# Spare transposes, a borrowed buffer and a new order in the setup of an adaptive-norm attention and expert block

## The chip, the core and the metric

The kernel runs on one core of a Trainium2 chip. The metric is the device time of one execution in microseconds (us). The engines are named as in the profile: PE is TensorE's matrix multiply and PEld its load of the stationary operand, DVE is VectorE, ACT is ScalarE, POOL is GpSimd, and SP is SyncE, whose queue (SPq) issues most transfers.

## What is computed

x is 2 x 2048 tokens of width 256. Everything is float32.

```
mod = (silu(c) @ wmod).reshape(B, 6, 1, 256)        # sa, ca, ga, sb, cb, gb
ga, gb = sign * max(abs, 0.25)
h   = layernorm(x) * (1 + ca) + sa
q, k, v = split(h @ Wqkv)                           # 16 heads of 64
p   = softmax(q k' / 8, each query sees itself and the 127 tokens before it)
x   = x + ga * ((p v) @ Wout)
h   = layernorm(x) * (1 + cb) + sb
the two best of 8 experts per token, at most 640 tokens per expert and choice:
y  += (relu(h W1[e] + b1[e]) W2[e] + b2[e]) * probability
x   = x + gb * y
```

## The kernel before, in words

**Split products.** Each float32 product is made of three matmuls in the fp32r format: a value is split into an upper part (a copy to fp32r, `upper` L129, on ACT) and a lower part (value minus upper, `lower` L133, on DVE or, for Wout, on POOL). `passes` (L225) multiplies upper by upper, upper by lower and lower by upper. So a weight is of use only once both parts are there.

**Setup.** SP loads c, the first x, the first third of wmod, and two of the six pieces of Wqkv (`weights` L359; piece n is q, k or v by n % 3, first or second half of the heads by n // 3). POOL writes the constants, ident for the transposes first. The setup makes silu(c) (sg, L436 to L439), transposes it (tp_c L442), multiplies it with wmod (`modulation` L451), copies the row to SBUF (wide, L464), and turns it to columns (mod_cols L469, cols L473). In the meantime `norm(0)` (L238), a generator moved on by `next(first)`, normalizes the first group (z), transposes it (tp_h L254), and scales it (hT L260) into its upper and lower part hh and hl.

**Pieces of weights.** Each `weights(n)` is a generator of three steps: load, `high(n)`, `low(n)`. The raw pieces share two buffers (tag raw of the pool stage), so the load of piece n+2 stands in `low(n)` (L388), behind the lower part that frees its buffer. Pieces 6 and 7 are the two halves of Wout.

**Attention.** A group is 256 tokens; there are 16, eight per batch. The 64 iterations of the loop (L1156) take two pairs of heads each, in a pipeline: iteration w makes q and k for the pairs of w+1 (`project_qk`), v (`project_v`), the scores of its own pairs (`scores`), packs them (`pack`), takes the maximum and the exponentials (`exps`); `normalize`, `turn`, `unpack`, `values` and `out_project` of a pair follow one to three iterations later. All matmul outputs of this part come from a ring of six PSUM banks (`bank`, L91), so a bank is written again only when the reader of the sixth output before it is done.

**Pack.** The scores of a head stand in one bank: per tile of 128 queries a block of own keys and a block of the keys before. In the first group of a batch (groups 0 and 8) the first tile has no keys before; DVE adds the mask `after` to it (L588). For the second tile ACT copies the own block (L595), and DVE copies over it, where the mask `within` says so, the block before (L596). Two heads make a pack, one bank each.

**Order.** Up to L1266 the order on every engine is the order of the program, written by hand. Work beside the pipeline is placed by strings such as "1A": iteration 1, point A. The points of an iteration are, in order, A, B, M, H, C, S, V (`go`, L1149). SECOND (L1108) places the rest of the setup (`second_half`, L491): the remaining weight pieces, the next x, the transposes of the gate weights (tp_g), the second and third part of the modulation with their rows (written to memory and read back, L531 to L535). `clear` (L537) writes zeros to the experts' buffers, two transfers per iteration of the first ones. After L1266 the order comes from a scheduler; there the experts run.

Of the kernel before, what the change touches and what calls it, by code (L numbers as in the profile page):

```python
# [8 lines left out]
FP = mybir.dt.float32  # L9
FR = mybir.dt.float32r  # L10
I32 = mybir.dt.int32
AF = mybir.ActivationFunctionType
ALU = mybir.AluOpType
# [4 lines left out]
P = 128  # L18
# [10 lines left out]
def adaln_block_kernel(  # L29
# [18 lines left out]
    nc = tc.nc  # L48
    B, S, D = x.shape
    DH = 64  # L50
    H = wqkv.shape[1] // 3 // DH
    HD = H * DH
# [7 lines left out]
    ND = D // P  # L60
# [6 lines left out]
    TS = SBT * P  # L67
# [20 lines left out]
    stage = ctx.enter_context(tc.tile_pool(name="stage", bufs=2))  # L88
    ring = {}

    def bank(name, shape=(P, 512)):  # L91
        return ring["pool"].tile(list(shape), FP, tag="ring", name=name, bufs=ring["bufs"])

    ident = const.tile([P, P], FP, name="ident")
# [26 lines left out]
            in_=rowd[b : b + 1, 0:3, :].rearrange("a i d -> a (i d)").to_broadcast([P, 3 * D]),  # L121
        )

    def load(src, shape, name):
        raw = stage.tile(shape, FP, tag="raw", name=f"raw_{name}")
        nc.sync.dma_start(out=raw, in_=src)
        return raw

# [62 lines left out]
    wq = bigw.tile([P, 2, ND, 3 * HD], FR, tag="big", name="wq")  # L191
# [8 lines left out]
    def load_x(g):  # L200
        xg = xp.tile([P, SBT, D], FP, tag="x", name=f"x_{g}")
        nc.sync.dma_start(
            out=xg, in_=xf[g * TS : (g + 1) * TS, :].rearrange("(t p) d -> p t d", p=P)
        )
        return xg
# [29 lines left out]

    qs, vs, xs, hs = {}, {}, {}, {}

    def norm(g):  # L238

        b = g // GPB  # L240
        xg = xs[g]
        mv, rs = norm_stats(xg, f"a{g}")
        yield
        z = wk.tile([P, SBT, D], FP, tag="t2", name=f"z_{g}")
        for t in range(SBT):
            nc.vector.tensor_scalar(
                z[:, t, :], xg[:, t, :], mv[:, t, 0:1], rs[:, t : t + 1],
                ALU.subtract, ALU.mult,
            )
        yield  # L250
        tp = bank(f"tp_h{g}")
        for k in range(ND):
            for t in range(SBT):
                nc.tensor.transpose(  # L254
                    tp[:, k * TS + t * P : k * TS + (t + 1) * P], z[:, t, k * P : (k + 1) * P], ident
                )
        yield
        hT = wk.tile([P, ND, TS], FP, tag="t2", name=f"hT_{g}")
        for k in range(ND):
            nc.vector.tensor_scalar(  # L260
                hT[:, k, :], tp[:, k * TS : (k + 1) * TS],
                cols[:, 1, k, b : b + 1], cols[:, 0, k, b : b + 1], ALU.mult, ALU.add,
            )
        hh = wk.tile([P, ND, TS], FR, tag="hh", name=f"hh_{g}")
        hl = wk.tile([P, ND, TS], FR, tag="hl", name=f"hl_{g}")
        if g:
            yield
            nc.scalar.copy(hh, hT)
            yield
        else:  # L270

            for k in range(ND):
                nc.scalar.activation(
                    hh[:, k, :], tp[:, k * TS : (k + 1) * TS], AF.Identity,
                    scale=cols[:, 1, k, b : b + 1], bias=cols[:, 0, k, b : b + 1],
                )
            yield
        nc.vector.tensor_tensor(hl, hT, hh, ALU.subtract)  # L278
        hs[g] = (hh, hl)
        yield  # L280
# [25 lines left out]
    def part(dh, dl, src):  # L306
        nc.scalar.copy(dh, src)
        nc.vector.tensor_tensor(dl, src, dh, ALU.subtract)  # L308
# [27 lines left out]
    first = norm(0)  # L336
# [7 lines left out]
    def load_mod(m):  # L344

        wms[m] = sp.tile([P, ND, 2 * D], FP, tag="wm", name=f"wm_{m}")
        nc.sync.dma_start(
            out=wms[m],
            in_=wmod.rearrange("(k p) f -> p k f", p=P)[:, :, 2 * m * D : (2 * m + 2) * D],
        )  # L350
# [3 lines left out]
    def columns(n):  # L354

        i, j = divmod(n, 3)
        return slice(j * HD + i * HD // 2, j * HD + (i + 1) * HD // 2)

    def weights(n):  # L359

        raw = load(
            wqkv[:, columns(n)].rearrange("(k p) f -> p k f", p=P), [P, ND, HD // 2], f"wq{n}"
        )
        hi, lo = (wq[:, m, :, columns(n)] for m in range(2))
        scale = None if n % 3 else QSCALE
        yield
        upper(hi, raw, scale)
        yield
        lower(hi, lo, raw, scale)
# [15 lines left out]
    def high(n):  # L385
        next(parts_[n])

    def low(n):  # L388

        next(parts_[n], None)  # L390
        if n + 2 < len(parts_):
            next(parts_[n + 2])

    for n in range(2):
        next(parts_[n])
# [42 lines left out]
    nc.vector.reciprocal(sg, sg)  # L438
    nc.vector.tensor_tensor(sg, sg, cr, ALU.mult)  # L439
    next(first)  # L440
    tp = bank("tp_c")
    nc.tensor.transpose(tp[:, 0 : B * ND], sg, ident[0 : B * ND, 0 : B * ND])  # L442
    scT = sp.tile([P, B, ND], FP, name="scT")
# [7 lines left out]
    def modulation(m):  # L451

        mr = bank(f"mod_{m}")
        for k in range(ND):
            nc.tensor.matmul(
                out=mr[0:B, :], lhsT=scT[:, :, k], rhs=wms[m][:, k, :],
                start=(k == 0), stop=(k == ND - 1),
            )
        return mr


    mr = modulation(0)
    wide2 = sp.tile([B, 2, D], FP, tag="wide", name="wide_0").rearrange("b i d -> b (i d)")
    nc.scalar.copy(wide2, mr[0:B, :])  # L464
    next(first)
    next(first)
    mc = bank("mod_cols")
    for i in range(2 * ND):
        nc.tensor.transpose(  # L469
# [9 lines left out]
    low(0)  # L479
    next(first)  # L480
    high(1)
    part(*project_qk(0, 0, 0))
    low(1)
    high(2)
    part(*project_qk(0, 0, 1))
    low(2)
# [4 lines left out]
    def second_half():  # L491

        for n in range(3, 8):
            if n == 5:
                load_mod(1)
            high(n)
            yield
            low(n)
            if n < 6:
                yield  # L500
        xs[2] = load_x(2)
        yield
        tp = bank("tp_g")
        for k in range(ND):
            nc.tensor.transpose(
                tp[:, k * E : (k + 1) * E], gw[:, k * P : (k + 1) * P], ident[0:E, 0:E]
            )
        nc.tensor.transpose(
            tp[:, ND * E : ND * E + E * NF], b1r, ident[0 : E * NF, 0 : E * NF]
        )  # L510
        nc.vector.tensor_copy(gwT.rearrange("p k e -> p (k e)"), tp[:, 0 : ND * E])
        nc.vector.tensor_copy(b1T, tp[:, ND * E : ND * E + E * NF])
        yield

        for g in range(2):
            mr = modulation(g + 1)
            if g == 0:
                load_mod(2)
            wide = sp.tile([B, 2, D], FP, tag="wide", name=f"wide_{g + 1}")
            gate, plain = (mr[0:B, 0:D], mr[0:B, D:]) if g == 0 else (mr[0:B, D:], mr[0:B, 0:D])  # L520
            nc.vector.tensor_scalar(sgn, gate, 0.0, 2.0, ALU.is_ge, ALU.mult)
            nc.vector.tensor_scalar(sgn, sgn, -1.0, None, ALU.add)
            nc.vector.tensor_tensor(mag, gate, sgn, ALU.mult)
            nc.vector.scalar_tensor_tensor(
                wide[:, g, :], mag, 0.25, sgn, ALU.max, ALU.mult
            )
            if g == 0:
                nc.vector.tensor_copy(wide[:, 1, :], plain)
            else:
                nc.vector.tensor_scalar(wide[:, 0, :], plain, 1.0, None, ALU.add)  # L530
            nc.sync.dma_start(out=rowd[:, 2 * g : 2 * g + 2, :], in_=wide)  # L531
            yield
        load_rows(0)
        for b in range(B):
            nc.sync.dma_start(out=gbr[:, b, :], in_=rowd[b, 3:4, :].to_broadcast([P, D]))  # L535
# [43 lines left out]
    def pack(g, hp):  # L579


        sc = scs.pop((g, hp))
        pm = wk.tile([P, 2, SBT, P], FP, tag="pm", name=f"pm_{g}_{hp}", bufs=4)
        first = g % GPB == 0
        for h in range(2):
            blocks = sc[h].rearrange("p t (n k) -> p (t n) k", n=2)
            if first:
                nc.vector.tensor_tensor(pm[:, h, 0, :], blocks[:, 1, :], after, ALU.add)  # L588
                ts, own, before = slice(1, 2), slice(3, 4), slice(2, 3)
            elif key_blocks(g, 0)[1]:  # L590
                ts, own, before = slice(0, 2), slice(0, 4, 3), slice(1, 3)
            else:
                ts, own, before = slice(0, 2), slice(1, 4, 2), slice(0, 4, 2)
            n = ts.stop - ts.start
            nc.scalar.copy(pm[:, h, ts, :], blocks[:, own, :])  # L595
            nc.vector.copy_predicated(  # L596
                pm[:, h, ts, :],
                within.rearrange("p (a k) -> p a k", a=1).to_broadcast([P, n, P]),
                blocks[:, before, :],
            )  # L600
        pms[g, hp] = pm

# [502 lines left out]
        NG - 2: "0H 1B 1V 2H 2C 2V 3A 3B 3H 3C 3V".split(),  # L1105
        NG - 1: ["0H"],
    }
    SECOND = "0B 0M 0M 0S 1B 1S 1V 2B 2V 3A 3A 3V 3V".split()  # L1108
    places = {}

    def place(work, w, at):
# [269 lines left out]
```

## Time and profile before

| | us |
|---|---|
| median of 3 runs | 1149.95 |
| lowest, highest | 1148.7, 1150.23 |
| the profiled execution, its time | 1148.45 |
| its span, first to last instruction | 1146.7 |
| PE busy | 1077.6 (94%) |
| PE weight loads busy | 991.4 (86%) |
| DVE busy | 874.0 (76%) |
| ACT busy | 678.0 (59%) |
| POOL busy | 587.0 (51%) |

The page gives the span in 40 slices of 28.7 us; a digit is the busy share of an engine in tenths, and the row PEclk is TensorE's granted clock in tenths of full speed. A line of the timeline is start, duration, engine, line of the kernel, operation, output <- inputs, shape and count, and in brackets how long the engine had been idle and what ended that. A line of the waits is the waiting instruction <- the one it waited for, with the sum in us, the number of waits and the longest. A line of the stretches is the stretch, its length, the busy time of PE, PEld, DVE, ACT and POOL with instruction counts, the granted clock, the DMA share and GB/s.

### The profile page before, as it was taken

Reading aid. Unit: us, or ns where it says so; the run is one execution under the profiler, and the core shown is the slowest. Engines: PE = TensorE matmul, PEld = TensorE weight load, DVE = VectorE, ACT = ScalarE, POOL = GpSimd, SP = SyncE. Lnnn points to the kernel's source line nnn. Section 1 sums busy time; section 2 is a strip of 40 time slices with the busy share of each in tenths; the row PEclk is TensorE's granted clock in tenths of the full one; section 3 lists DMA queues with packets and bytes.
Section 4 is the critical chain, followed back from the end, with each engine's and each line's share of the span. In section 5 each row is a group of like instructions: output and inputs, shape, how many; then the busy total and the mean of one; then the engine's idle time right before and its main releaser. Section 6 shows DMA issues by size and latency. Waiting matters only on the chain. (4 is left out here: it accounts for less than half of the span.)

```text
span 1146.7 us, 25186 instructions
## 1 busy us (share of the span) xinstructions
PE 1077.6 (94%) x9238; PEld 991.4 (86%) x9238; DVE 874.0 (76%) x2170; ACT 678.0 (59%) x2099; POOL 587.0 (51%) x767
## 2 busy tenths in 40 slices
PE   6799999999999999999999997788899999999995
PEld 4589999999999889999999996678799999999994
DVE  4667778878878778888888876677678787778773
ACT  3667677777777577777777776433444444344441
POOL 1345375575575555665665666444233525443524
PEclk9899999999999999999999998779999999999998
DMA  4866200000000010010010022233353434343413
GB/s 130 205 147 152 45 30 20 31 30 20 30 30 21 21 48 25 21 36 20 18 36 21 18 61 66 76 99 90 70 140 94 64 106 87 87 83 76 76 50 37
DMA packets 59863, 72.09 MB, mean 63 GB/s; under 512 B 4841, under 2 KB 51186, under 8 KB 59728
## 3 DMA queue, kind: packets, MB, share of 16 engines
q1 hardware_dynamic: 48016, 55.54, 17.1%
q0 software_dynamic: 11712, 14.79, 7.5%
q8 instruction: 80, 1.31, 0.5%
q14 instruction: 55, 0.45, 0.1%
HBM read 40.11 MB, written 32.27 MB: 63 GB/s over the span
## 5 line engine op out<-in xcount | busy, mean ns | idle before, releaser
L230 PE MATMUL pq<-hh,wq 128*128 128x256 f32 x1024 | 217.9, 297 | 7.8 <-DVE wq L135 5.4
L1008 ACT ACTIVATE hm<-ph,b1T 128x256 fp32r<-128x256 f32 (+2 forms) x184 | 99.2, 539 | 212.3 <-PE ph L230 182.3
L619 ACT ACTIVATE pm<-pm,mx 128x128 f32<-128x128 f32 x512 | 204.3, 403 | 15.7 <-DVE mx L605 15.6
L230 PE MATMUL y<-we,hm 128*128 128x256 f32 x1440 | 203.1, 285 | 6.2 <-DVE hm L1010 6.1
L230 PE MATMUL ph<-xT,we 128*128 128x256 f32 (+2 forms) x1104 | 199.2, 320 | 9.0 <-PEq L1314 3.6
L230 PEld LDWEIGHTS y<-we,hm 128*128 128x128 f32 x1440 | 186.9, 190 | 9.6 <-DVE hm L1010 8.3
L653 POOL TENSOR_SCALAR_AFFINE_SELECT pT<-pT 128x512 f32<-128x512 f32 (+1 forms) x128 | 79.8, 624 | 207.1 <-ACT pT L652 207.0
L230 PEld LDWEIGHTS ph<-xT,we 128*128 128x128 f32 x1104 | 168.2, 192 | 13.9 <-issue 4.2
L230 PEld LDWEIGHTS pq<-hh,wq 128*128 128x128 f32 x1024 | 170.8, 194 | 10.3 <-DVE wq L135 5.8
L230 PE MATMUL pq<-hl,wq 128*128 128x256 f32 x512 | 146.7, 287 | 0.6 <-DVE hl L278 0.6
L1009 DVE TENSOR_SCALAR r<-ph,b1T 128x256 f32<-128x256 f32 (+2 forms) x184 | 102.5, 563 | 58.6 <-ACT hm L1008 49.4
L629 POOL TENSOR_TENSOR pm<-pm,rd 128x512 f32<-128x512 f32 x128 | 133.6, 1044 | 26.0 <-DVE rd L627 26.0
L595 ACT COPY pm<-sc 128x256 f32<-128x256 f32 (+1 forms) x256 | 81.0, 362 | 107.0 <-PE sc L571 72.5
L1073 POOL TENSOR_TENSOR ys<-ys,gw 128x256 f32<-128x256 f32 x56 | 47.4, 942 | 171.3 <-DVE ys L1063 168.6
L676 PE MATMUL av<-pT,v 128*64 128x128 f32 (+1 forms) x1472 | 124.5, 317 | 5.2 <-ACT v L326 1.8
L676 PEld LDWEIGHTS av<-pT,v 128*64 128x64 f32 x1472 | 89.7, 138 | 33.2 <-issue 3.5
L596 DVE COPY_PREDICATED pm<-within,sc 128x256 f32<-128x256 int32 (+1 forms) x256 | 96.1, 422 | 24.9 <-ACT pm L595 23.8
L1074 POOL DMA_INDIRECT out_dram<-ys,tok x60 | 97.2, 1620 | 28.0 <-issue 12.1
L571 PE MATMUL sc<-kr,qh 64*128 64x256 f32 (+1 forms) x1024 | 102.5, 294 | 1.4 <-DVE ql L308 1.2
L230 PEld LDWEIGHTS pq<-hl,wq 128*128 128x128 f32 x512 | 99.6, 195 | 0.9 <-DVE hl L278 0.9
L619 ACT ACTIVATION_READ_ACCUMULATOR pm<-pm,mx 128x1 f32 x512 | 99.8, 195 | 0.0
L1010 DVE TENSOR_TENSOR hm<-r,hm 128x256 fp32r<-128x256 f32 (+2 forms) x144 | 95.2, 661 | 5.4
(166 smaller groups left out, 2249.5 us busy)
## 6 DMA issues: line engine op xcount, KB each, us to landing
raw_w<-in_L_ffn_W_dram SPq DMA_DIRECT2D x32, 512.0 KB, 3.7
xbuf<-blank SPq DMA_DIRECT2D x16, 685.0 KB, 10.1
xt<-xbuf SPq DMA_DIRECT2D x7, 822.0 KB, 6.5
xt<-xbuf SPq DMA_DIRECT2D x8, 548.0 KB, 4.9
x<-in_L_attn_x_dram SPq DMA_DIRECT2D x16, 256.0 KB, 2.9
out_dram<-x SPq DMA_DIRECT2D x16, 256.0 KB, 2.2
raw_wq<-in_L_attn_Wqkv_dram SPq DMA_DIRECT2D x6, 512.0 KB, 4.1
wm<-in_L_wmod_dram SPq DMA_DIRECT2D x3, 512.0 KB, 5.3
```

The lines of the kernel that those rows point to most:

```text
L230: nc.tensor.matmul(out=out_, lhsT=a, rhs=b, start=start and n == 0 and i == 0, stop=stop and n == last and i == 2, **kw,)
L571: nc.tensor.matmul(out=sc[h][:, t, lo:], lhsT=q[r, t * P : (t + 1) * P], rhs=kr[r, (0, 1, 0)[i], hp, blk, :], start=(i == 0), stop=(i == 2),)
L595: nc.scalar.copy(pm[:, h, ts, :], blocks[:, own, :])
L596: nc.vector.copy_predicated(pm[:, h, ts, :], within.rearrange("p (a k) -> p a k", a=1).to_broadcast([P, n, P]), blocks[:, before, :],)
L619: nc.scalar.activation(pm[:, h, t, :], pm[:, h, t, :], AF.Exp, bias=mx[:, h, t : t + 1], accum_out=den[:, h, t : t + 1],)
L629: nc.gpsimd.tensor_tensor(pmv, pmv, rd.rearrange("p h (t a) -> p (h t) a", a=1).to_broadcast([P, 2 * SBT, P]), ALU.mult,)
L653: nc.gpsimd.affine_select(out=pT[:, :, t0:, 0, :], in_=own[:, :, t0:, :], pattern=[[0, 2], [0, n], [-1, P]], compare_op=ALU.is_gt, fill=0. ...
L676: nc.tensor.matmul(out=av[h * DH : (h + 1) * DH, q0 : q0 + hi - lo], lhsT=v[:, f0 + h * DH : f0 + (h + 1) * DH], rhs=pT[:, h, lo:hi], star ...
L1008: nc.scalar.activation(hh[:, s], phv, AF.Relu, bias=bias)
L1009: nc.vector.tensor_scalar(r[:, s], phv, bias, 0.0, ALU.add, ALU.max)
L1010: nc.vector.tensor_tensor(hl, r[:, 0:W], hh, ALU.subtract)
L1074: add = nc.gpsimd.indirect_dma_start(out=of, out_offset=bass.IndirectOffsetOnAxis(ap=tok[:, 0:1], axis=0), in_=y, in_offset=None, bounds_c ...
```

## The change

1. `keep_warm(n)` issues n transposes of ident on TensorE into a bank that nothing reads: 11 before tp_c, 3 before the modulation's matmul, 4 before mod_cols, 12 before the first projection.
2. Piece 2 of Wqkv (v, first half) is loaded into the buffer of the first third of wmod, behind the modulation's matmul, no longer behind `low(0)`. So `low(0)` loads piece 3, `low(1)` piece 4, and from `low(3)` on it is piece n+2 as before.
3. `low(1)` moves ahead of the first pair's `part`: on DVE ahead of ql_0. `low(4)` moves from point S of iteration 0 to point C: on DVE ahead of its packs.
4. wide is copied by DVE, no longer by ACT. For the first group hh is copied from hT by ACT, no longer computed by ACT from the bank that DVE reads for hT.
5. In a pack, the copy of ACT is issued first, and DVE's mask add goes to the other head's bank; both predicated copies stand at the end. In other groups than a batch's first, the order on each engine stays as it was.
6. The third x is loaded in iteration 1, ahead of the load of wmod. The second half of Wout (upper and lower part) moves from iteration 2 to 3, the lower part of its first half from point B to H of iteration 2, the gate transposes and the second part of the modulation from iteration 3 to 4, the third part and the rows from iteration 3 to 5. Clears and rows change places on SP accordingly.

PE's, DVE's, ACT's and POOL's orders differ nowhere else in the hand-ordered part but for the packs of group 8; in the scheduled part about ten matmuls change places with neighbours.

```diff
--- before.py
+++ after.py
@@ -121,8 +121,8 @@
             in_=rowd[b : b + 1, 0:3, :].rearrange("a i d -> a (i d)").to_broadcast([P, 3 * D]),
         )
 
-    def load(src, shape, name):
-        raw = stage.tile(shape, FP, tag="raw", name=f"raw_{name}")
+    def load(src, shape, name, pool=stage, tag="raw"):
+        raw = pool.tile(shape, FP, tag=tag, name=f"raw_{name}")
         nc.sync.dma_start(out=raw, in_=src)
         return raw
 
@@ -235,6 +235,12 @@
 
     qs, vs, xs, hs = {}, {}, {}, {}
 
+    def keep_warm(n):
+
+        tp = bank("idle")
+        for i in range(n):
+            nc.tensor.transpose(tp[:, i % 4 * P : (i % 4 + 1) * P], ident, ident)
+
     def norm(g):
 
         b = g // GPB
@@ -256,6 +262,8 @@
                 )
         yield
         hT = wk.tile([P, ND, TS], FP, tag="t2", name=f"hT_{g}")
+        if g == 0:
+            keep_warm(12)
         for k in range(ND):
             nc.vector.tensor_scalar(
                 hT[:, k, :], tp[:, k * TS : (k + 1) * TS],
@@ -268,12 +276,8 @@
             nc.scalar.copy(hh, hT)
             yield
         else:
-
             for k in range(ND):
-                nc.scalar.activation(
-                    hh[:, k, :], tp[:, k * TS : (k + 1) * TS], AF.Identity,
-                    scale=cols[:, 1, k, b : b + 1], bias=cols[:, 0, k, b : b + 1],
-                )
+                nc.scalar.copy(hh[:, k, :], hT[:, k, :])
             yield
         nc.vector.tensor_tensor(hl, hT, hh, ALU.subtract)
         hs[g] = (hh, hl)
@@ -359,7 +363,8 @@
     def weights(n):
 
         raw = load(
-            wqkv[:, columns(n)].rearrange("(k p) f -> p k f", p=P), [P, ND, HD // 2], f"wq{n}"
+            wqkv[:, columns(n)].rearrange("(k p) f -> p k f", p=P), [P, ND, HD // 2], f"wq{n}",
+            *((sp, "wm") if n == 2 else ()),
         )
         hi, lo = (wq[:, m, :, columns(n)] for m in range(2))
         scale = None if n % 3 else QSCALE
@@ -388,8 +393,8 @@
     def low(n):
 
         next(parts_[n], None)
-        if n + 2 < len(parts_):
-            next(parts_[n + 2])
+        if n != 2 and n < 6:
+            next(parts_[n + (3 if n < 2 else 2)])
 
     for n in range(2):
         next(parts_[n])
@@ -438,6 +443,7 @@
     nc.vector.reciprocal(sg, sg)
     nc.vector.tensor_tensor(sg, sg, cr, ALU.mult)
     next(first)
+    keep_warm(11)
     tp = bank("tp_c")
     nc.tensor.transpose(tp[:, 0 : B * ND], sg, ident[0 : B * ND, 0 : B * ND])
     scT = sp.tile([P, B, ND], FP, name="scT")
@@ -459,11 +465,14 @@
         return mr
 
 
+    keep_warm(3)
     mr = modulation(0)
+    next(parts_[2])
     wide2 = sp.tile([B, 2, D], FP, tag="wide", name="wide_0").rearrange("b i d -> b (i d)")
-    nc.scalar.copy(wide2, mr[0:B, :])
     next(first)
+    nc.vector.tensor_copy(wide2, mr[0:B, :])
     next(first)
+    keep_warm(4)
     mc = bank("mod_cols")
     for i in range(2 * ND):
         nc.tensor.transpose(
@@ -479,8 +488,8 @@
     low(0)
     next(first)
     high(1)
+    low(1)
     part(*project_qk(0, 0, 0))
-    low(1)
     high(2)
     part(*project_qk(0, 0, 1))
     low(2)
@@ -492,14 +501,12 @@
 
         for n in range(3, 8):
             if n == 5:
+                xs[2] = load_x(2)
                 load_mod(1)
             high(n)
             yield
             low(n)
-            if n < 6:
-                yield
-        xs[2] = load_x(2)
-        yield
+            yield
         tp = bank("tp_g")
         for k in range(ND):
             nc.tensor.transpose(
@@ -582,10 +589,10 @@
         sc = scs.pop((g, hp))
         pm = wk.tile([P, 2, SBT, P], FP, tag="pm", name=f"pm_{g}_{hp}", bufs=4)
         first = g % GPB == 0
+        late = []
         for h in range(2):
             blocks = sc[h].rearrange("p t (n k) -> p (t n) k", n=2)
             if first:
-                nc.vector.tensor_tensor(pm[:, h, 0, :], blocks[:, 1, :], after, ALU.add)
                 ts, own, before = slice(1, 2), slice(3, 4), slice(2, 3)
             elif key_blocks(g, 0)[1]:
                 ts, own, before = slice(0, 2), slice(0, 4, 3), slice(1, 3)
@@ -593,10 +600,16 @@
                 ts, own, before = slice(0, 2), slice(1, 4, 2), slice(0, 4, 2)
             n = ts.stop - ts.start
             nc.scalar.copy(pm[:, h, ts, :], blocks[:, own, :])
+            late.append((h, ts, n, blocks[:, before, :]))
+            if first:
+
+                blocks = sc[1 - h].rearrange("p t (n k) -> p (t n) k", n=2)
+                nc.vector.tensor_tensor(pm[:, 1 - h, 0, :], blocks[:, 1, :], after, ALU.add)
+        for h, ts, n, blocks in late:
             nc.vector.copy_predicated(
                 pm[:, h, ts, :],
                 within.rearrange("p (a k) -> p a k", a=1).to_broadcast([P, n, P]),
-                blocks[:, before, :],
+                blocks,
             )
         pms[g, hp] = pm
 
@@ -1105,7 +1118,7 @@
         NG - 2: "0H 1B 1V 2H 2C 2V 3A 3B 3H 3C 3V".split(),
         NG - 1: ["0H"],
     }
-    SECOND = "0B 0M 0M 0S 1B 1S 1V 2B 2V 3A 3A 3V 3V".split()
+    SECOND = "0B 0M 0M 0C 1B 1S 1V 2H 3H 3V 4A 4A 5A 5A".split()
     places = {}
 
     def place(work, w, at):
```

## The prediction

> **What bounds the kernel now.** I read the page's slices first, then the granted clock and busy time in stretches, then the start in order of time, then the waits there.
>
> ```profile
> PE   6799999999999999999999997788899999999995
> PEclk9899999999999999999999998779999999999998
> ```
>
> ```profile
> 35.00:38.20 3.20, 3.20 (x12) 2.63 (x11) 1.95 (x4) 3.20 (x11) 2.03 (x2) 0.52 0.83 222
> 52.10:55.30 3.20, 3.20 (x21) 2.20 (x17) 2.12 (x7) 0.80 (x3) 3.20 (x3) 0.51 1.11 267
> ...
> 390.00:400.00 10.00, 8.76 (x81) 7.57 (x79) 8.62 (x29) 7.04 (x27) 4.20 (x6) 1.00 0.00 0
> 400.00:410.00 10.00, 8.49 (x68) 7.35 (x65) 6.51 (x19) 6.74 (x27) 2.90 (x5) 1.00 0.08 28
> ```
>
> TensorE is full nearly everywhere: what the change can win is the first two slices (57 us), and a dent at 390 to 430 us, the second batch's first group. In the stretches (busy PE, PEld, DVE, ACT, POOL, clock, DMA) the clock is halved at 35 and at 52 us.
>
> ```profile
> 12.93 0.58 PE L230 MATMUL pq<-hh,wq 128*128 128x256 f32 x1 [2.01 <-ACT hh L273]
> ...
> 19.36 0.80 PE L230 MATMUL pq<-hh,wq 128*128 128x256 f32 x2 [2.10 <-DVE wq L135]
> ...
> 24.65 0.52 PE L230 MATMUL pq<-hh,wq 128*128 128x256 f32 x2
> ...
> 34.19 0.50 PE L230 MATMUL pq<-hh,wq 128*128 128x256 f32 x2 [3.25 <-DVE wq L135]
> ...
> 51.80 2.49 PE L676 MATMUL av<-pT,v 128*64 128x256 f32 x16 [1.43 <-ACT v L326]
> ```
>
> The five marks of the start. The projection's matmuls follow each other every 0.213 us up to 24.65 and every 0.12 us after (their start times), so the clock is half until 24.65, though the clock column says 1.00 there. Twice TensorE waits for a weight's lower part (2.1 and 3.25 us), and at 51.80 for ScalarE's v. After 51.80 it is never idle before the dent.
>
> ```profile
> 31.28 0.28 DVE L588 TENSOR_TENSOR pm<-sc,after 128x128 f32<-128x128 f32 x1
> 31.89 0.30 DVE L596 COPY_PREDICATED pm<-within,sc 128x128 f32<-128x128 int32 x1 [0.33 <-ACT pm L595]
> 32.10 0.28 DVE L588 TENSOR_TENSOR pm<-sc,after 128x128 f32<-128x128 f32 x1
> ```
>
> The next line is from the waits of the first 70 us (total, times, longest).
>
> ```profile
> ACT pm L595 <- DVE pm L588: 12.6, 15, 1.4
> ```
>
> One pack of a first group: add, ScalarE's copy, predicated copy, one after the other on one bank, then the same on the other bank. Each handover is 0.31 us start to start.
>
> **Step 1, setup to the first projection: +0.6 us.** Eleven transposes start once ident is there (1.38). At half clock four transposes of this shape took 1.11 us (tp_h at 9.29), pitch 0.22: 11 x 0.22 = 2.4, over before the vector sg ends at 4.47 (without that cover they would cost their 2.4). The next three (0.7) end by 5.6, before the modulation's matmul, which starts at 5.79 on wm's landing: nothing. Its four take 3.57 at half clock (1.88 in the later ones at full). Four more stand ahead of mod_cols: 10.15 + 0.9 = 11.05 instead of 10.34, +0.7; VectorE's copy of wide (0.41 for 256 columns, so about 0.7) hides under them (alone it is 0.1 more than ScalarE's 0.57). Then hT at 11.9 (before 11.22). The last twelve run 11.6 to 14.2 at 0.213, while hT, wq's lower part and hl (0.99 + 1.21 + 0.69, serial on VectorE) end at 14.7: hidden. If VectorE were faster they would cost up to 1.3. hh as a copy of hT replaces two activations (1.02) and doesn't bind. First full pair at 14.7, before 14.11: +0.6. If the clock opens inside the setup, modulation alone gives back 1.7: bounds -2 and +2.
>
> **Step 2, the 2.1 us stall: gone.** Lower(1) now stands ahead of ql_0 on VectorE, at 14.7 to 15.9; the second half of the q,k projection wants it later. ql_0 waits behind it, but its qh isn't ready before 17; were it ready, ql_0 and the packs after it would be 1.2 late.
>
> **Step 3, the clock.** The half stretches begin and end at 34.9, 38.3, 52.0, 55.4; with 24.65 these are multiples of 3.41 us apart. The Trainium skill (TensorE: Matmul & The Clock Gate, Part 1) has such a window, free-running, so its phase differs in each execution. Against the change stands Part 4, PE-mode transpose, of that page: transposes don't count as busy for the clock. The row: in the window 51.96 to 55.37 matmuls fill only 66% (av to 54.2), transposes of 1.12 us nearly all the rest, and full clock came at its end; the window 14.41 to 17.82, 83% matmul and then idle, didn't open it. I follow the row; the thin modulation (2 columns) probably counts for little, since 7.6 to 11.0 was full and opened nothing. Counting from the twelve at 11.6, the first full window ends between 15.0 and 18.4, say 16.7: of 48 projection matmuls 9 run at 0.213 and 39 at 0.12, 14.75 + 1.95 + 4.7 = 21.4. Before, they ended at 25.95: 4.5 gained so far (steps 1 to 3). By the skill's rule only projection matmuls count, the window closes about 19.9, 24 run slow, and they end at 22.8: 1.4 less.
>
> **Step 4, to the scores of pairs 2 and 3.** The third weights (v) land in wm's freed buffer: issued at 9.4, landing 4.1 to 5.7 later, needed at 17.6. That load makes SP wait for the modulation; behind it stand only the loads that wait for low(0) at 14.0 anyway. SP's next loads wait for low(0), low(1), low(3), low(4) as listed in the built order; 4.1 each lands them ahead of use. On ScalarE: qh, high(2) 1.05, kr, qh, high(3), kr, v, high(4) from 17.1 give 24.4; VectorE's low(4), 1.22, ends at 25.7 and the packs begin, before at 28.5: 2.8 earlier. What was queued behind VectorE's low(4), the packs, pays 1.2 at the front but saves it in the middle. Then the same chain as before (pack, maximum, pack, maximum, exps, high(5), kr): 10.5 us from 28.52 to 39.04. It loses low(4) from its middle (1.1) and 0.6 per pack: by the 0.31 handovers a pack reaches its maximum after 1.17 instead of 1.78. So 8.2, and the scores go at 33.9, before 38.96: 5.1. The 3.25 stall is gone, but TensorE now waits on this chain, about 28.9 to 33, and the clock will drop once more near 32 to 35.
>
> **Step 5, to the first values.** 12.84 before, from 38.96 to 51.80. Off it: two packs 1.2, ScalarE's second copy of wo (0.95) moved to the fourth iteration; on it: up to 0.8 for scores at half clock, taken 0.4. So 33.9 + 11.1 = 45.0: 6.8 earlier. The half clock at 52 goes with the idle ahead of it: av 2.49 to 1.52, tp 1.12 to 0.66, 1.4 more: 8.2.
>
> **Step 6, later.** TensorE is full from there, so what moves later (gate transposes, two modulations at 1.88, wo's lower parts on POOL, 2.35 each, clears and rows on SP) keeps its sum. The fourth iteration lacks these 4.3 us as cover: ScalarE's work there, 8 x 0.39 + two pT + qh, kr, v + four copies + ah, about 8 us plus wo's 1.05, stands against TensorE's 9.7. Thin: I take 0.5 loss (0 to 1.5). x for group 2 moves ahead of the modulation load on SP; used an iteration later.
>
> **Step 7, the second batch's first group.** Idle there 1.24 + 1.51 + 0.82 + 0.20 = 3.8. Eight packs save 4.9 on VectorE's chain, and ScalarE's copies no longer stand up to 3.3 us behind VectorE. Bounds 0 and 3.8; TensorE waits there for pm and v, rows that the packs delay, so I take 2.3.
>
> **Sum.** 8.2 - 0.5 + 2.3 = 10.0. The profiled execution took 1148.45 (span 1146.7 and 1.75 around it): 1138.45. The median of the runs is 1.5 above it: 1140.0.
>
> **Rivals.** A, chance 0.56: as summed, 1140. B, 0.15: transposes don't open the clock. 1.4 lost in step 3: 1141.4. C, 0.15: packs don't shorten, since ScalarE's own order paces them: 1.2 + 1.2 + 2.3 lost, 1144.7; for it, ScalarE is full at 44 to 48; against it, it waits 12.6 us for VectorE's add. D, 0.09: the clock opens within the setup and the chain follows: 1137. E, 0.05, slower: the gate rows. The second modulation moves to the sixth iteration, about 69 to 71; wide on VectorE to 75, written and read back through memory (3.8 and 3.6 to landing), rows at 83. Close(0)'s first product would want them at about 87 (before 95.5, and VectorE is in order: packs and kr queue behind it). SP has two clears ahead of the write, 10.1 us to landing. If they hold it over 4 us, each further us is lost; from 14 us the kernel is slower: 1153.
>
> A measurement here can tell about 0.2%, 2.3 us. Faster 0.92, same 0.04 (0.03 of C, 0.01 of E), slower 0.04 (E). Range 1136 to 1145.5: step 1's early clock and step 7's 3.8 below, C above.
>
> **What would show it.** Right: no wait for wq's lower part over 0.5; 0.12 pitch from 15 to 18.5; scores of pairs 2 and 3 near 34, first values near 45; ScalarE's wait for VectorE's add nearly gone; stretches 380 to 425 fuller. Wrong: pitch 0.213 past 19, a new VectorE wait for rows, TensorE idle in the fourth and fifth iteration.

## The result and the profile after

The changed kernel takes 1138.39 us (median of 4 runs, 1136.84 to 1140.53) where the kernel before took 1150.09 beside it (1148.7 to 1150.56): ratio 0.9902, interval 0.9881 to 0.9922. That is 11.7 us between the medians, 11.3 by the ratio. The forecast was 1140.0. Its profiled execution took 1137.36, with a span of 1135.6 (before 1148.45 and 1146.7).

The slices of the page after, as before in tenths of 28.4 us each:

```profile
PE   8999999999999999999999996788899999999995
...
PEclk9899999999999999999999998889999999999998
```

The first two slices read 8 and 9 where they read 6 and 7; the slices of the experts, from the 25th on, keep their shape to within one digit. The stretches after (busy PE, PEld, DVE, ACT, POOL with counts, clock, DMA share, GB/s):

```profile
12.80:19.40 6.60, 5.63 (x47) 5.63 (x48) 4.69 (x7) 3.73 (x6) 0.00 (x0) 1.00 0.55 159
...
380.00:420.00 40.00, 38.56 (x358) 34.90 (x358) 32.64 (x103) 28.71 (x105) 24.95 (x36) 1.00 0.11 39
```

The same 40 us before, with the dent in it:

```profile
380.00:420.00 40.00, 36.43 (x319) 31.97 (x318) 29.77 (x91) 24.68 (x96) 18.82 (x28) 1.00 0.10 31
```

These two stretches are the same in time, not in work. The same work, from ScalarE's 32nd copy of v to its 41st, is 896 matmuls in both kernels. Here it is before, and then in a second execution of the changed kernel (after_again, below):

```profile
362.18:462.83 100.65, 96.75 (x896) 86.64 (x895) 82.08 (x243) 68.31 (x249) 60.58 (x85) 1.00 0.09 30
...
350.58:447.04 96.46, 94.74 (x896) 86.05 (x895) 81.31 (x243) 68.44 (x250) 60.38 (x85) 1.00 0.10 31
```

It takes 4.2 us less. TensorE's idle time is 2.2 us of that (3.90 to 1.72), its busy time the other 2.0 (96.75 to 94.74), with the same matmuls at the same clock: so short stalls between matmuls are booked as busy, and the dent is worth more than TensorE's idle time in it.

TensorE after, in order of time:

```profile
1.44 2.61 PE L242 MATMUL idle<-ident 128*128 128x128 f32 x11 [1.44 <-POOL ident masks.py:199]
...
6.23 3.09 PE L461 MATMUL mod<-wm,scT 128*2 128x512 f32 x4 [0.61 <-DMA wm<-in_L_wmod_dram]
9.25 0.66 PE L260 MATMUL tp_h<-ident,z 128*128 128x128 f32 x4
9.74 0.60 PE L242 MATMUL idle<-ident 128*128 128x128 f32 x4
...
10.61 1.53 PE L242 MATMUL idle<-ident 128*128 128x128 f32 x12
12.02 0.39 PE L230 MATMUL pq<-hh,wq 128*128 128x256 f32 x1
13.77 0.39 PE L230 MATMUL pq<-hl,wq 128*128 128x256 f32 x1 [1.36 <-DVE hl L282]
...
29.09 0.86 PE L260 MATMUL tp_h<-ident,z 128*128 128x128 f32 x3 [0.66 <-DVE z L252]
29.89 0.69 PE L578 MATMUL sc<-kr,qh 64*128 64x128 f32 x4
...
41.68 1.52 PE L689 MATMUL av<-pT,v 128*64 128x256 f32 x16 [0.39 <-ACT v L330]
```

The same marks of before, but for the values at 51.80, which the prediction shows:

```profile
14.11 0.58 PE L230 MATMUL pq<-hl,wq 128*128 128x256 f32 x1 [0.60 <-DVE hl L278]
...
38.96 0.44 PE L571 MATMUL sc<-kr,qh 64*128 64x128 f32 x4
```

The first hl stood at 14.11, the scores of pairs 2 and 3 at 38.96 and the first values at 51.80; they are now 13.77, 29.89 and 41.68. The modulation's four matmuls are partly at full clock already (3.09 instead of 3.57), the transposes of z take 0.66 instead of 1.11. Both waits for a weight's lower part are gone.

VectorE's packs after:

```profile
23.80 0.48 DVE L607 TENSOR_TENSOR pm<-sc,after 128x128 f32<-128x128 f32 x2
24.20 0.52 DVE L609 COPY_PREDICATED pm<-within,sc 128x128 f32<-128x128 int32 x2
24.75 0.69 DVE L618 TENSOR_REDUCE mx<-pm 128x4 f32<-128x512 f32 x1
```

The adds of both banks run back to back, then both predicated copies: first add to maximum 0.95 us. In the waits of the first 70 us, ScalarE's copy for VectorE's add (total, times, longest) is down from 12.6, 15, 1.4:

```profile
ACT pm L602 <- DVE pm L607: 6.9, 7, 1.3
```

How far ahead the changed kernel is can be followed by ScalarE's copies of v, one per iteration, in the two profiled executions: 6.45 us at the first (27.54 to 21.09), 10.1 at the third, 11.5 at the ninth (115.23 to 103.76), 10.8 at the 33rd (372.75 to 361.93), 14.6 behind the dent, at the 41st (462.83 to 448.27), 14.0 at the end of the attention (ScalarE's 14th copy h2T, 731.82 to 717.82), 11.1 at the program's end. These marks serve in all experiments below.

Not all of the first 6.45 us belongs to the change. The run pack_only, below, has the setup of before without an edit. Its first hl matmul and its first copy of v, and then those copies of before and after:

```profile
13.34 0.58 PE L230 MATMUL pq<-hl,wq 128*128 128x256 f32 x1 [0.60 <-DVE hl L278]
...
25.97 0.59 ACT L326 COPY v<-pv 128x512 f32<-128x512 f32 x1 [0.80 <-PE pv L230]
...
27.54 0.59 ACT L326 COPY v<-pv 128x512 f32<-128x512 f32 x1 [0.80 <-PE pv L230]
...
21.09 0.58 ACT L330 COPY v<-pv 128x512 f32<-128x512 f32 x1 [0.80 <-PE pv L230]
```

The 1.6 us between the two executions of one setup come from TensorE's clock. In the profiled execution of before it was half up to 24.65; in that of pack_only it was full from 8.6 to 12.1 and again from 22.3. Beside pack_only's, the lead at the first copy of v is 4.9 us.

### The profile page after: what moved, and what is told of

It is laid out like the page before. It is cut to its first block, busy times and chain, and to the rows that moved or that the text cites. A ratio compares the mean times of both kernels' runs of the same rounds, so it can differ in the third digit from the quotient of the medians.

```text
span 1135.6 us, 25259 instructions
## 1 busy us (share of the span) xinstructions
PE 1073.5 (95%) x9268; PEld 990.8 (87%) x9268; DVE 872.8 (77%) x2171; ACT 677.7 (60%) x2098; POOL 588.5 (52%) x767
## 5 line engine op out<-in xcount | busy, mean ns | idle before, releaser
L230 PE MATMUL pq<-hh,wq 128*128 128x256 f32 x1024 | 214.6, 293 | 0.0
L230 PEld LDWEIGHTS pq<-hh,wq 128*128 128x128 f32 x1024 | 168.4, 192 | 2.0 <-DVE b1T L519 0.9
```

Source lines behind the costliest of these rows:

```text
L230: nc.tensor.matmul(out=out_, lhsT=a, rhs=b, start=start and n == 0 and i == 0, stop=stop and n == last and i == 2, **kw,)
```

## The experiments

All are the changed kernel with one part undone, except warm_only and pack_only, which are the kernel before with one part added, and the last three, which go further. "Cost" is the difference of a kernel's ratio from that of after_again (0.9894, interval 0.9880 to 0.9908), times 1148 us; its uncertainty is the root of the two squared half widths. (Taken from the first runs' ratio, 0.9902, each cost would be 0.9 us lower.)

The profiled executions also differ in when TensorE's clock opened. In those that keep the setup of after (after, after_again, old_pack, old_low, shared_buf, old_late) it opened between 8.7 and 10.9, and the first hl matmul starts between 13.60 and 14.51. So up to 0.9 us of a shift of the marks is this, not the part undone; the times are medians of several executions.

**after_again**: the changed kernel once more, without an edit. In the first profile of after, each group of the attention had lost about 0.13 us, and the question was whether that belongs to the kernel.

> The changed kernel once more, beside the others of this call. v of the first pairs at 21.1 us, of the third iteration at 41.0, as before. Open: its first profile is 11.5 us ahead at 85 us, but loses 0.13 once per group (scores to values 0.34 instead of 0.21), 1.5 in all, and 2.9 in the experts. Theory (a fixed wait of this program): the same loss per group. Rival (an accident of that execution): gone, so that 15 us are left at the end of the attention.

It does not: ahead by 11.59 us at 104 and at 340 us, 16.3 at the end of the attention, 14.7 at the end; 1134.81 against 1147.77. Two executions of one kernel thus differ by 2 to 4 us behind the first 100 us; the marks up to there repeat to 0.15 us in these two, which both had the clock open at about 8.7.

**no_warm**: no transposes.

```
-            keep_warm(12)
...
-    keep_warm(11)
...
-    keep_warm(3)
...
-    keep_warm(4)
```

> The changed kernel without the 30 unread transposes; all else stays. Theory: they open the clock. Without them it opens with the first full stretch of 3.4 us of projection, between 16.4 and 19.8 us, so some 24 of the first 48 projection matmuls run at a pitch of 0.213 us instead of 0.12: v of the first pairs is 2 us later than its 21.1, and the time is about 1140.5. Rival (transposes don't count as busy, the modulation's matmuls opened the clock): the clock opens in the setup as before, 1138.4 or 0.5 less, for the four transposes ahead of mod_cols are gone.

In its stretches, behind the setup:

```profile
12.80:19.40 6.60, 5.79 (x27) 5.79 (x28) 2.58 (x4) 2.41 (x4) 0.00 (x0) 0.50 0.51 159
```

27 matmuls at half clock where after has 47 at full. Yet the clock had opened without transposes, at 9.3, at the end of the modulation; it fell back from 12.7 to 19.6. The first copy of v is 2.44 us late (23.53), the ninth 2.7: the 2 us that I expected, but by a clock that opened and fell again, not by one that opened late. In the time this is not to be seen: 1135.64 against 1147.86, ratio 0.9885 (0.9866 to 0.9904), cost -1.0 +- 2.7.

**first14**: the 14 transposes of the setup stay, the last 16 go.

```
-            keep_warm(12)
...
-    keep_warm(4)
```

> The changed kernel with only the 14 transposes ahead of the modulation. Theory: the clock opens near 8.7 us as now, but TensorE is nearly idle from 10 to 13.8, so it falls back for a window, and v of the first pairs comes at about 23.5, as without any transposes: 1140 at most, and the last 16 are what holds the clock. Rival (the clock, once open, stays): 21.1, 1138.4.

First copy of v at 23.46, the clock opened at 9.2 and fell from 12.6 to 19.5, all as in no_warm. So in these executions the first 14 do nothing, and the last 16 do all there is. 1137.02 against 1147.77, ratio 0.9903 (0.9890 to 0.9916), cost +1.0 +- 2.2.

**warm_only**: the kernel before with the 30 transposes at the same four places.

```
+        if g == 0:
+            keep_warm(12)
...
+    keep_warm(11)
...
+    keep_warm(3)
...
+    keep_warm(4)
```

> The kernel before with the 30 unread transposes alone. Theory: the clock opens in the setup, the projections of the first pairs end near 22 instead of 25.95 and the packs start 3.5 earlier: 1146.5. Rival (the waits for the weights' lower parts take the gain): 1149 or more.

1149.08 against 1147.86, ratio 1.0006 (0.9994 to 1.0019): nothing gained, and my expectation fell. The first copy of v (25.18) comes 2.4 us sooner than before, but only 0.8 sooner than in pack_only, which has no added transposes. TensorE then waits as long as before for the lower parts of two weights (2.30 and 3.21 us; 2.1 and 3.25 before), only sooner, and behind both the second copy of v is still 2.3 us ahead. So my rival, that these waits take the gain, has the number right but not the place. At the third copy 0.6 us is left, at the fourth and ninth it is 0.2 behind. Where it went:

```profile
49.02 1.04 ACT L131 CAST wo<-raw_wo 128x1024 fp32r<-128x1024 f32 x1 [1.67 <-DMA raw_wo<-in_L_attn_Wout_dram]
...
51.18 2.83 PE L687 MATMUL av<-pT,v 128*64 128x256 f32 x16 [3.22 <-ACT v L334]
```

ScalarE comes to the second half of Wout before it has landed. Its load was issued at 42.88 and it copies at 49.02, after a wait; before, the load was issued at 45.28 and ScalarE copied at 49.65 without one. v stands behind that copy, TensorE waits 3.22 us for v (1.43 before), and its clock is half from 49.6 to 56.5, where the first values fall (2.83 us; 2.49 before). This is the wait that old_late, below, meets too, and that the change takes away by moving the copy. Why the load took 6.1 us here and at most 4.4 before is open.

**old_pack**: the new kernel with the pack of before.

```
-        late = []
...
+                nc.vector.tensor_tensor(pm[:, h, 0, :], blocks[:, 1, :], after, ALU.add)
...
-            late.append((h, ts, n, blocks[:, before, :]))
-            if first:
-                blocks = sc[1 - h].rearrange("p t (n k) -> p (t n) k", n=2)
-                nc.vector.tensor_tensor(pm[:, 1 - h, 0, :], blocks[:, 1, :], after, ALU.add)
-        for h, ts, n, blocks in late:
...
-                blocks,
+                blocks[:, before, :],
```

> The changed kernel with the pack of before (add, copy and predicated copy of one bank, then of the other). Theory: the dent at 380 to 430 us comes back, 4.2 us, and each of the first iterations' two packs is 1.2 longer on VectorE's chain, 2.4 together: about 1145. Rival (TensorE has slack there, the gain in the dent came from elsewhere): 1138.4 to 1140.

1143.92 against 1147.86, ratio 0.9959 (0.9945 to 0.9973): cost 7.5 +- 2.3. The ninth copy of v is 5.5 us later than in after_again (0.6 of it already at the first, ahead of any pack), the end of the attention 10.2. The wait in the first 70 us is back, and so is the dent:

```profile
ACT pm L602 <- DVE pm L595: 13.0, 15, 1.5
```

```profile
380.00:420.00 40.00, 37.03 (x329) 32.39 (x326) 31.70 (x101) 24.36 (x92) 17.57 (x28) 0.96 0.07 24
```

**pack_only**: the kernel before with the new pack; the edit above, reversed.

> The kernel before with the new pack alone. Theory: the dent of the second batch's first group closes by 4.2 to 4.7 us, as in the changed kernel, and each of the first iterations' two packs takes 1.2 less on VectorE's chain, 2.4 to the first values: 7 in all, 1141 beside 1147.8. Rival (at the start the weights' lower parts still set the pace): the dent's 4.5 alone, 1143.3. Rival (the pack gains only together with the earlier weights): 1146 or more.

1144.11 against 1149.76, ratio 0.9947 (0.9934 to 0.9961): 6.1 us gained. In the trace 2.3 us are there at the third copy of v, but 1.6 of these already at the first, ahead of any pack. That leaves 0.8 for the packs at the start, where I expected 2.4: there the first rival is nearer. The dent gives 3.4 (1.5 ahead at the 32nd copy, 5.0 at the 41st); 4.0 us are there at the end of the attention. The dent is full:

```profile
380.00:420.00 40.00, 38.55 (x363) 34.56 (x363) 33.40 (x107) 27.73 (x102) 22.09 (x33) 1.00 0.10 28
```

With the rest of the change alone (old_pack, 4.7 us below its kernel before) this makes 10.8; the whole gave 11.3 and 12.2. In time the packs and the rest add up, within the intervals. At the start they do not, in these executions: undone in the changed kernel, the packs cost 4.9 us up to the ninth copy of v (with a half clock from 44.2 to 47.6, which may be part of it), and added alone to the kernel before they bring 0.8.

This run also gave the cleanest view of the clock. Its setup is that of before, its clock opened at 8.6 in this execution, behind a window with nothing in it but the modulation's matmuls, and warm_only's at 8.7: the same window, the same setup, with and without the last 16 transposes. First pack_only, then warm_only:

```profile
5.20:8.60 3.40, 2.81 (x4) 0.37 (x4) 1.11 (x5) 0.00 (x0) 1.35 (x4) 1.00 0.98 352
8.70:12.10 3.40, 1.36 (x9) 0.74 (x8) 1.89 (x5) 2.10 (x4) 0.00 (x0) 0.99 0.08 25
```

```profile
8.70:12.10 3.40, 3.38 (x26) 2.47 (x24) 1.40 (x5) 1.61 (x3) 0.00 (x0) 1.00 0.04 12
12.10:15.50 3.40, 2.06 (x14) 1.80 (x14) 1.65 (x2) 1.93 (x4) 0.00 (x0) 1.00 0.30 87
```

At 12.1 pack_only fell to half and stayed there to 22.3; warm_only kept the full clock, and kept it again behind the next window with 2.06 us busy, until 18.9. (Where the column reads 1.00 ahead of its first fall, the opening is told from the length of the matmuls and by counting back in steps of 3.41 us from a later edge: in after, the half stretch from 29.2 to 36.0 is two steps long, and six steps back from 29.2 is 8.7.)

**old_low**: the lower parts back in their old places.

```
-    low(1)
     part(*project_qk(0, 0, 0))
+    low(1)
...
-    SECOND = "0B 0M 0M 0C 1B ..."
+    SECOND = "0B 0M 0M 0S 1B ..."
```

> The changed kernel with the lower parts of pieces 1 and 4 where they were before. Theory: TensorE waits again for piece 1, from 15.2 to about 17.7, and piece 4's 1.2 us stands among the packs again: about 3.4 later, 1141.8. Rival (the chain of packs and exponentials sets the pace, so earlier weights are only waited for elsewhere): within 0.5 of 1138.4.

1137.82 against 1147.86, ratio 0.9908 (0.9890 to 0.9926), cost 1.6 +- 2.6, which does not settle it. The trace does for its part: copies of v are 2.9 later at the second and third, 4.5 at the ninth, of which 0.9 stood at the first hl matmul already (14.51; the clock opened at 10.9). And TensorE waits where it did before:

```profile
18.62 0.50 PE L230 MATMUL pq<-hh,wq 128*128 128x256 f32 x2 [2.29 <-DVE wq L135]
```

**shared_buf**: piece 2 of Wqkv waits for a stage buffer again.

```
-            *((sp, "wm") if n == 2 else ()),
...
-        if n != 2 and n < 6:
-            next(parts_[n + (3 if n < 2 else 2)])
+        if n + 2 < len(parts_):
+            next(parts_[n + 2])
...
-    next(parts_[2])
```

> The changed kernel with the third piece in the shared buffers again, so every later piece's load waits for one lower part more. Theory: piece 2 lands at 17.2, its lower part and v are 1.2 later; piece 4 is loaded behind the lower part of piece 2 (20.7) and lands at 24.8, 3.2 later than ScalarE takes it now, and the packs queue behind its lower part: v of the second iteration 3.2 later, 1141.6. Rival (loads have slack): 1138.4 and no shift over 0.5.

1137.81 against 1147.77, ratio 0.9921 (0.9905 to 0.9937), cost 3.1 +- 2.4. The second copy of v is 2.9 us later and the ninth 3.0 (0.5 of it at the first hl matmul already), near what was expected, since ScalarE's upper parts wait for their landing:

```profile
17.19 1.05 ACT L131 CAST wq<-raw_wq 128x1024 fp32r<-128x1024 f32 x1 [0.89 <-DMA raw_wq<-in_L_attn_Wqkv_dram]
...
24.33 1.05 ACT L131 CAST wq<-raw_wq 128x1024 fp32r<-128x1024 f32 x1 [1.65 <-DMA raw_wq<-in_L_attn_Wqkv_dram]
```

**old_late**: Wout's second half, the gate transposes and the modulations in their old iterations.

```
-                xs[2] = load_x(2)
...
-            yield
+            if n < 6:
+                yield
+        xs[2] = load_x(2)
+        yield
...
-    SECOND = "0B 0M 0M 0C 1B 1S 1V 2H 3H 3V 4A 4A 5A 5A".split()
+    SECOND = "0B 0M 0M 0C 1B 1S 1V 2B 2V 3A 3A 3V 3V".split()
```

> The changed kernel with the late setup (second half of Wout, gate transposes, modulations, third x) placed in iterations 2 and 3 as before, only piece 4's lower part stays ahead of the packs. Theory: ScalarE's second copy of Wout stands ahead of kr and v of the third iteration again, v there 0.95 later; with a half clock behind that wait up to 1.4 more: 1139.3 to 1140.8. Rival (TensorE sets the pace there): 1138.4.

1140.02 against 1147.77, ratio 0.9932 (0.9919 to 0.9945), cost 4.4 +- 2.2. The second copy of v is 0.8 late, as the first hl matmul was; the third is 3.3 late. ScalarE:

```profile
42.62 1.04 ACT L131 CAST wo<-raw_wo 128x1024 fp32r<-128x1024 f32 x1 [1.40 <-DMA raw_wo<-in_L_attn_Wout_dram]
...
44.05 0.59 ACT L330 COPY v<-pv 128x512 f32<-128x512 f32 x1
```

and TensorE:

```profile
44.78 2.83 PE L691 MATMUL av<-pT,v 128*64 128x256 f32 x16 [2.38 <-ACT v L330]
```

With everything else sooner, the second half of Wout (issued at 36.74) has not landed when ScalarE comes to copy it, as in warm_only. The copy stands ahead of v in ScalarE's order, so TensorE idles 2.38 us for v, and its values then run at half clock (2.83 instead of 1.52).

**low0_early**: further than the change: the split of the first weight ahead of the first scaling (hT, hh) on ScalarE and VectorE, wide back on ScalarE.

```
-    nc.vector.tensor_copy(wide2, mr[0:B, :])
     next(first)
+    high(0)
+    low(0)
+    nc.scalar.copy(wide2, mr[0:B, :])
...
-    high(0)
     next(first)
-    low(0)
```

> The changed kernel, with the lower part of piece 0 ahead of cols and hT on VectorE, where it sits idle for 2 us behind z, and wide copied by ScalarE again, idle there. Theory: hl ends 1.1 earlier, so the first projections start at 12.7 instead of 13.8, and the chain of ScalarE and VectorE follows: v of the first pairs at 19.9, 1133.7 beside 1134.8. Rival (a load or the clock's phase takes it): within 0.3 at v.

Inconclusive: 1137.84 against 1149.76, ratio 0.9898 (0.9883 to 0.9912). The first copy of v came at 21.26, no sooner. In this execution the clock opened only at 10.7, and hl now waits for ScalarE's hh:

```profile
13.19 0.69 DVE L282 TENSOR_TENSOR hl<-hT,hh 128x512 fp32r<-128x512 f32 x1 [0.47 <-ACT hh L280]
```

**ahead**: low0_early, and besides z of group 1 moved to point V of iteration 0, off TensorE's wait of 1.05 and 0.66 us for z, and ScalarE's copy of piece 5 moved from point B to M of iteration 1, behind kr and v.

```
-    SECOND = "0B 0M 0M 0C 1B 1S 1V ..."
+    SECOND = "0B 0M 0M 0C 1M 1S 1V ..."
...
-            place(norm(g), (g - 1) * (NP // 2), NORM)
+            place(norm(g), (g - 1) * (NP // 2), NORM if g > 1 else ["0B", "0V", *NORM[2:]])
```

> As the run before this one, and two more steps taken off the chain: z of the second group ahead of the first reciprocal (TensorE's transposes wait for it from 27.1 to 29.1), and ScalarE's copy of piece 5 behind kr and v of the second iteration. Theory: 1.1 + 0.6 + 0.95 = 2.6 less at the third iteration's v, 38.2 instead of 40.8; 1132.2. Rival (what is waited for next is the half clock of TensorE from 29 to 36): only 1.1 to 1.5 less.

Here the clock opened at 8.3, and the first hl matmul starts at 12.78, the first copy of v at 20.10, close to the 12.7 and 19.9 expected of low0_early. The second and third copy of v are 1.8 us sooner than in after_again, the ninth 0.5. 1137.69 against 1149.76, ratio 0.9890 (0.9873 to 0.9907): not to be told from after_again. A half-clock window took most of it:

```profile
39.75 2.83 PE L689 MATMUL av<-pT,v 128*64 128x256 f32 x16 [0.41 <-ACT v L330]
```

In after the half clock lies at 29.2 to 36.0. ScalarE is busy there from 34.3 to 41.7 without a break, and TensorE still waits 0.39 us for its v, so what the half clock cost there cannot be read. Here it lies at 39.1 to 42.5, on the values (2.83 instead of 1.52).

**ahead_hold**: ahead, and twelve transposes ahead of tp_h of group 1, to hold the clock through that stretch.

```
+        if g == 1:
+            keep_warm(12)
         tp = bank(f"tp_h{g}")
```

> As ahead, with 12 unread transposes before the second group's transposes, where TensorE is idle. Theory: they hold the clock, so the 6.8 us at half clock from 29 to 36 go; TensorE is not alone on the path there, so up to 1.5 less at the third iteration's v than in ahead. Rival (ScalarE's and VectorE's chain sets the pace): no half clock, but the same v.

The half clock came all the same, at 41.9 to 45.3. None stood between 29 and 36, but ahead had none there either, so this shows nothing of the twelve. The clock opened at 11.2, the first copy of v came 1.4 later than in ahead, the third at 40.42. 1138.43 against 1149.76, ratio 0.9905 (0.9890 to 0.9920). No version was found that beats the changed kernel by more than the intervals.

## Why the prediction was right, and where its steps were not

The direction, the size and the main mechanism held: a setup and first iterations bound by chains of small steps, shortened at several places, then a full TensorE that keeps the gain. Step by step:

1. **Setup, +0.6 predicted, -0.3 measured** (13.77 against 14.11). The added transposes are hidden as said. But the clock opened at 8.7, inside the setup, so modulation and transposes ran faster. This is rival D's mechanism, within the bounds given. It is not the change's doing: in pack_only, with the setup of before, the clock opened at 8.6 and the first hl matmul stands at 13.34. Like for like the setup is 0.4 longer, as the sum had it; that 13.77 lies below 14.11 is luck.
2. **The 2.1 us stall: gone**, as said. old_low brings it back (2.29).
3. **The clock: right effect, wrong reason.** I let the transposes open it at about 16.7, and took the modulation's thin matmuls for little. (I had also read its edges about 0.2 us early: the half stretches of before are 35.1 to 38.5 and 52.2 to 55.6.) It opened at 8.7, and without the last 16 transposes it opened at 8.6 to 9.3 (pack_only, no_warm, first14): the modulation opens it. In before it did not; its windows ended at about 7.8 and 11.2 (35.1 less eight and seven times 3.41) and cut the modulation in two, which I take for the reason. What the transposes do is hold it open until the projections begin, and only the last 16 do it (first14). The rule of the Trainium skill (TensorE: Matmul & The Clock Gate, Part 4, PE-mode transpose), as rival B took it, would have let the clock fall at 12.1 in warm_only as in pack_only; it did not. Whether transposes also help to open it is not settled. For it: in ahead_hold the modulation was cut in mid-window too, transposes filled the rest (3.40 of 3.40 us busy from 7.8 to 11.2), and the clock opened at 11.2; old_low is alike, at 10.9. Against it: the like stretch of before, 7.85 to 11.25, with 3.07 us busy and four transposes among it, opened nothing, while 2.81 us of modulation sufficed in pack_only. Gain up to here: 6.45 instead of 4.5, of which 1.6 is the late clock of the profiled execution of before; 4.9 beside pack_only's.
4. **Scores of pairs 2 and 3: 33.9 predicted, 29.89 measured.** This is the step that failed. I let them wait for the same chain as before (packs, maxima, exponentials, kr). They need only q and k of the second projection, which were there; the chain behind them had been setting their start only because TensorE was late itself. Now TensorE waits 1.05 and 0.66 us for z, which stands on VectorE behind the packs, the maxima and a reciprocal that waits for ScalarE's first exponentials: a chain of the same kind, but one that ends sooner. The packs did begin early (23.80, predicted 25.7) and shorten more than said (0.95 from add to maximum; 1.17 predicted). The clock dropped once more as predicted, but for twice as long: 29.2 to 36.0, where 32 to 35 was said. ScalarE's wait for VectorE's add was to be nearly gone; 6.9 of 12.6 us are left.
5. **First values: 45.0 predicted, 41.68 measured**; 10.1 sooner instead of 6.8. From the scores on it gained 1.0 (the lead there was 9.1), where 1.7 was predicted, so a part of step 4's surplus was lost again. The full clock there gave its 1.4 (values 1.52): 11.5 at the ninth copy of v against 8.2.
6. **Loss in the fourth and fifth iteration: 0.5 predicted, none measured.** TensorE has no wait between 45 and 90 us. The move itself is worth more than the 0.95 that I booked: 4.4 in old_late, for the landing of Wout and the half clock behind it, which only exist because TensorE is sooner; warm_only lost its lead to the same wait. The gate rows of rival E were issued at 71.6 and first used at 84.0, and nobody waited.
7. **The dent: 2.3 predicted, about 4.2 measured** (11.6 to 15.8 ahead in after_again; 11.0 to 14.6, 3.6, in after). I bounded it by the idle time of TensorE there, 3.8. Of the 4.2, idle time is 2.2; the other 2.0 are stalls booked as busy, which I had put at nothing. Rival C, that ScalarE paces the packs, is refuted by pack_only: 6.1 us (4.5 to 7.6) from the packs alone.

So the terms were mis-sized low by 4 us in all: 10.0 predicted, 14.0 at the end of the attention, 1.6 of which is the clock of before. What I had not foreseen is that 2.9 of that (1.6 in after_again) were given back in the experts. From the mark at the end of the attention to the program's end it took 414.9 us before, 417.8 in after, 416.6 in after_again, and 417.1 in warm_only, whose edit lies in the setup. Of all 14 profiles before is the lowest, 419.2 (old_pack) the highest. So I take the loss for variation between executions, with a quick one in the profile of before; it is not shown, and in this part about ten matmuls of the changed kernel stand elsewhere. That 1140.0 came within 1.6 us of the time is thus in part luck: terms too small, and a loss that was not foreseen.

By experiments with one part undone, the gain lies in the packs (7.5 +- 2.3), the late moves (4.4 +- 2.2), the freed buffer (3.1 +- 2.4) and the order of the lower parts (1.6 +- 2.6, not clear of noise); these overlap and need not sum to 12. Item 4 of the change (wide on VectorE, hh from hT) was not undone alone. The transposes, named first in the change, bring 2.4 us in the trace at the start, and alone they bring nothing (warm_only). Open: why those 2.4 us, still there at 100 us in no_warm, do not show in its time; its interval allows up to 1.7 of cost, first14's up to 3.2. A spread of 2 us between executions at the end of the attention is what stands in the way.

## What to carry to other kernels

A warm clock is worth only what the next wait leaves of it: keep it warm when the data are on time, and first get the data on time. Two engines that take turns on one PSUM bank pay for each handover; give both engines two banks to alternate on, and look for stages that do so more than once. Before a mark of one profiled execution is booked as gain, see whether the clock opened at the same time in both: here that alone was 1.6 us. When a kernel's start is bound by several chains, each mark has to be checked against what it truly needs, not against the chain that ended last when everything was late.

## What the runs showed of the hardware that was not expected

- Four matmuls with 2 columns of stationary operand (the modulation, 2.81 of 3.40 us busy in pack_only) open the clock. In 13 of the 14 profiles it opened at 8.3 to 11.2, in the other (before) at 24.65; pack_only and before have the same setup and fall on either side.
- Transposes that nobody reads hold it: 26 instructions with 3.38 us busy kept it, 9 with 1.36 us did not, in the same window of the same setup; a window with 2.06 us kept it too.
- Half-clock spells last 3.4 us, twice or three times that (10.2 in pack_only), at places that differ between executions and versions: 29.2 to 36.0 in after, 39.1 to 42.5 in ahead. On the values such a spell costs 1.3 us (2.83 instead of 1.52).
- The same 896 matmuls at full clock took 96.75 us of busy time in one kernel and 94.74 in the other.
